# Layer norm sums over partitions on GpSimd instead of a fold, a split and a product, and a ScalarE/GpSimd mix for the first tile's receptance

## The chip, the cores and the metric

The kernel runs on one NeuronCore of a Trainium2 chip. The metric is the device time of one execution in microseconds (us); the median of three runs of the kernel before is 1569.22 us (1567.82 to 1571.45). TensorE multiplies matrices into PSUM, VectorE and ScalarE do elementwise work, GpSimd does elementwise work on SBUF and issues DMAs, and SyncE only issues DMAs. Each engine executes its own instructions in the order in which they were built.

## The reference, cut to what matters

The input x is [2, 4096, 256]. Features lie on partitions (two blocks of 128), time on the free axis. The block is a layer norm, an RWKV attention, a second layer norm and a gated feed-forward of four weight matrices:

```python
def _layernorm(x, axis=-1, eps=1e-05):
    m = jnp.mean(x, axis=axis, keepdims=True)
    v = jnp.var(x, axis=axis, keepdims=True)
    return (x - m) / jnp.sqrt(v + eps)
...
xr = x * time_mix_r + x_prev * (1.0 - time_mix_r)      # likewise xk, xv
r = jax.nn.sigmoid(jnp.einsum('btd,ed->bte', xr, W_r))  # likewise k, v
y = r * _wkv_scan(k, v, time_decay, time_first)
x = x + jnp.einsum('btd,ed->bte', y, W_o)
...
h = silu(lin(z, w1)) * lin(z, w2)          # z = layernorm(x), 256 -> 1024
h = gelu(lin(h, h1)); h = gelu(lin(h, h2))  # 1024 -> 1024, twice
x = x + lin(h, w3)                          # 1024 -> 256
```

Since features lie on partitions, the mean and the variance of a layer norm are sums over partitions.

## The kernel before, in words

There are 16 tiles of 512 time steps. The feed-forward `ffn(i)` of tile i is woven with the attention of tile i+1 (`attention`) and the first layer norm of tile i+2 (`normalise`): all are generators, and the main loop advances them step by step. A scheduler of the framework then gives each engine its final order. The first tile has a hand-written order instead (`first_tile`): `on(...)` puts every instruction behind the last one of its engine.

Feed-forward products are split: each activation is a rounded part `hi` and a rest `lo`, and every weight block is multiplied by both (lines 172 and 173). A first-layer block f makes two PSUM tiles `pa` and `pb`. ScalarE applies Silu to `pa` (L564), VectorE multiplies by `pb` (`gated`, L565), ScalarE rounds (`hi`, L179) and VectorE subtracts (`lo`, L180). PSUM pool `ps_ffn` has four buffers, so `pb` of block f+2 takes the buffer of `pb` of block f and can start only when L565 of block f has read it. In the two middle layers ScalarE reads PSUM twice (L580, L582) and VectorE makes `lo` (L583).

A layer norm takes two partition sums, each made by `average` in five instructions: VectorE adds the two feature blocks (`both`, L187); ScalarE moves the upper 64 partitions down (`folded`, L189); VectorE adds the halves (L192); ScalarE rounds (`hi` of `parts`, L194) and VectorE makes the rest (L197); then one product with a matrix of 1/256 (L201) gives the average in every partition, in PSUM. Then L212 subtracts the mean, L215 squares, a second `average` and L218 give the standard deviation, L220 the reciprocal, L222 the product.

There are four such sums in every tile but the first, 60 in all. The first tile has its own layer norm (`first_layernorm`), and it scales the weights (`scaled`) so that its k, v and r projections need no mixed input: each takes four products per half of the features.

GpSimd's queue issues the casting weight loads at the start, `h2` to a rounded copy in HBM in eight pieces and `w3` among them (L123, L124), the loads of x (L95), the stores of the output (L604) and the loads for comparing the rounded weights (L152).

Of the kernel before, what the change touches and what calls it, by code (L numbers as in the profile page):

```python
# [7 lines left out]

F32 = mybir.dt.float32
F32R = mybir.dt.float32r  # L10
# [3 lines left out]
P = 128  # L14
B, T, D, HID = 2, 4096, 256, 1024
TS = 512
# [49 lines left out]
def split_block(ctx, tc, flags, x, vecs, w_attn, w1, w2, h1, h2, w3, out):  # L66
# [52 lines left out]
    h2_hbm = dram.tile([NH, P, NH, P], F32R, name="h2_hbm")  # L119
    for sb, src in ((w1_sb, w1), (w2_sb, w2), (h1_sb, h1)):  # L120
        nc.gpsimd.dma_start(out=sb, in_=src)
    for f in range(NH):
        nc.gpsimd.dma_start(out=h2_hbm[f], in_=h2[:, :, f * P : (f + 1) * P])  # L123
    nc.gpsimd.dma_start(out=w3_sb, in_=w3)  # L124

    mean_w = const.tile([P, P], F32, name="mean_w")
    vector.memset(mean_w, 1.0 / D)
# [51 lines left out]
        marks["rounded"] = scalar.activation(hi, full, AF.Copy)  # L179
        marks["rest"] = vector.tensor_tensor(lo, full, hi.bitcast(F32), ALU.subtract)  # L180

    def average(a, b, tag, name, pause=False):

        both = one.tile([P, TS], F32, tag=tag, name="both")
        marks["both"] = vector.tensor_tensor(both, a, b, ALU.add)  # L187
        folded = one.tile([P // 2, TS], F32, tag="folded", name="folded")
        marks["shift"] = scalar.activation(folded, both[P // 2 :, :], AF.Copy)  # L189
        if pause:  # L190
            yield
        marks["fold"] = vector.tensor_tensor(folded, folded, both[: P // 2, :], ALU.add)  # L192
        parts = one.tile([P, TS], F32R, tag="parts", name="parts")
        marks["hi"] = scalar.activation(parts[: P // 2, :], folded, AF.Copy)  # L194
        if pause:
            yield
        marks["split"] = vector.tensor_tensor(parts[P // 2 :, :], folded, parts[: P // 2, :].bitcast(F32), ALU.subtract)  # L197
        if pause:
            yield
        psum = ps_sum.tile([P, TS], F32, tag="ps", name=name)  # L200
        marks["average"] = tensor.matmul(psum, mean_wr, parts, start=True, stop=True)  # L201
        return psum

    def layernorm(src, new_xc, tag, pause=False):


        mean = yield from average(src[:, 0, :], src[:, 1, :], tag, "mean", pause)
        if pause:
            yield
        xc = new_xc()  # L210
        for h in range(ND):
            vector.tensor_tensor(xc[:, h, :], src[:, h, :], mean, ALU.subtract)  # L212
        yield
        sq = wide.tile([P, ND, TS], F32, tag="wide", name="sq")
        scalar.activation(sq, xc, AF.Square)  # L215
        var = yield from average(sq[:, 0, :], sq[:, 1, :], tag, "var")
        rstd = one.tile([P, TS], F32, tag=tag, name="rstd")
        scalar.activation(rstd, var, AF.Sqrt, bias=eps)  # L218
        yield
        vector.reciprocal(rstd, rstd)  # L220
        for h in range(ND):
            vector.tensor_tensor(xc[:, h, :], xc[:, h, :], rstd, ALU.mult)  # L222
        yield
# [126 lines left out]
    def add(out, a, b, op=ALU.add):  # L350
        on("vector", "tensor_tensor", out, a, b, op)

    def load_sqrt_table():
        activation(root, eps, AF.Sqrt)

    def keep_warm(unread, n, size=TS):

# [6 lines left out]
    def first_layernorm(src, xc, means):  # L364

        sq = wide.tile([P, ND, TS], F32, tag="wide", name="sq")
        for mean, p in zip(means, halves):
            for h in range(ND):  # L370
                add(xc[:, h, p], src[:, h, p], mean, ALU.subtract)
            activation(sq[:, :, p], xc[:, :, p], AF.Square)
        varis = []
        for p in halves:
            add(sq[:, 0, p], sq[:, 0, p], sq[:, 1, p])
            var = ps_ffn.tile([P, TS // 2 // P], F32, tag="pf", name="var")
            for b in range(TS // 2 // P):
                t = slice(p.start + b * P, p.start + (b + 1) * P)
                matmul(var[:, b : b + 1], sq[:, 0, t], mean_w[:, 0:1], start=True, stop=True)
            varis.append(var)  # L380
        yield
        spread = []
        for var in varis:
            each = tmp.tile([P, TS // 2 // P], F32, tag="each", name="each")
            activation(each, var, AF.Sqrt, bias=eps)
            on("vector", "reciprocal", each, each)
            rstd = ps_ffn.tile([P, TS // 2], F32, tag="pf", name="rstd")
            for b in range(TS // 2 // P):
                matmul(
                    rstd[:, b * P : (b + 1) * P], each[:, b : b + 1].to_broadcast([P, P]), ident, start=True, stop=True  # L390
                )
            spread.append(rstd)
            yield
        for rstd, p in zip(spread, halves):
            for h in range(ND):
                add(xc[:, h, p], xc[:, h, p], rstd, ALU.mult)
            yield

    def first_tile(second):
# [13 lines left out]
                    both = one.tile([P, 2, TS], F32, tag=tag, name="scale")  # L413
                    scales.append([both[:, k, :] for k in range(2)])

        load_sqrt_table()
        unread = ps_sum.tile([P, TS], F32, tag="ps", name="unread")
        keep_warm(unread, 8)
        means = []
# [6 lines left out]
        norm = first_layernorm(x_sb, xn, means)  # L426


        scaled = [[hid.tile([P, ND, D], F32, tag=tag, name="ws") for tag in ("hi", "lo")] for m in range(3)]

        def scale(m, *which):
            for k, c in which:
# [1 line left out]
                activation(scaled[m][k][:, c, :], wa_sb[:, m, c, :], AF.Copy, scale=(vec, unmix)[k][:, j : j + 1])  # L434

        next(norm)
        scale(0, (0, 0))
        next(norm)
        scale(0, (1, 0))
        next(norm)  # L440
        scale(0, (1, 1), (0, 1))
        for m in range(1, 3):
            scale(m, (0, 0), (1, 0), (1, 1), (0, 1))
        run(norm)
        nc.gpsimd.tensor_copy(prev, xn[:, :, TS - 1 :])

        def project(m, h, kind, p=whole):
            pool, tag = kind
            ps = pool.tile([P, p.stop - p.start], F32, tag=tag, name="ps_" + "kvr"[m])
            now, then = (ws[:, :, h * P : (h + 1) * P] for ws in scaled[m])  # L450
            skip = 1 if p.start == 0 else 0
            shifted = slice(p.start + skip - 1, p.stop - 1)
            matmul(ps, now[:, 0, :], xn[:, 0, p], start=True, stop=False)
            for c in range(ND):
                matmul(ps[:, skip:], then[:, c, :], xn[:, c, shifted], start=False, stop=False)
            matmul(ps, now[:, 1, :], xn[:, 1, p], start=False, stop=True)
            return ps
# [6 lines left out]
        def differences(h):  # L464
# [5 lines left out]
                on("vector", "scalar_tensor_tensor", sc[h][1][:, p], t, w, k, ALU.add, ALU.subtract)  # L470
                on("vector", "scalar_tensor_tensor", so[h][1][:, p], k, u, t, ALU.add, ALU.subtract)
            on("vector", "tensor_scalar", sc[h][0], sc[h][1], NEG_CLAMP, 0.0, ALU.max, ALU.min)
            nc.gpsimd.tensor_copy(log_max[:, h : h + 1], lm[h][:, TS:])

        def scales(h):
            activation(sc[h][0], sc[h][0], AF.Exp)
            activation(sc[h][1], sc[h][1], AF.Relu)
            activation(sc[h][1], sc[h][1], AF.Exp, scale=-1.0)

        def state(h):  # L480

            on("vector", "scalar_tensor_tensor", sc[h][1], sc[h][1], MIN_SCALE, v[h], ALU.max, ALU.mult)
            on("vector", "tensor_tensor_scan", num[h][:, 1:], sc[h][0], sc[h][1], num[h][:, 0:1], ALU.mult, ALU.add)
            nc.gpsimd.tensor_copy(numer[:, h : h + 1], num[h][:, TS:])
            for share, of in zip(so[h], (num[h][:, 0:TS], v[h])):
                on("vector", "scalar_tensor_tensor", share, share, MIN_SHARE, of, ALU.max, ALU.mult)
            add(so[h][0], so[h][0], so[h][1])

        differences(0)
        with behind("vector"), behind("scalar"):  # L490
            next(second)
        last["vector"], last["scalar"] = marks["both"], marks["shift"]
        scales(0)
        with behind("vector"), behind("scalar"):
            next(second)
        last["vector"], last["scalar"] = marks["fold"], marks["hi"]
        differences(1)
        scales(1)
        for h in range(ND):
            activation(so[h][0], so[h][1], AF.Sigmoid, scale=-1.0)  # L500
            activation(so[h][1], so[h][1], AF.Sigmoid)
        for h in range(ND):
            activation(r[h], r[h], AF.Sigmoid)
            state(h)
        load_sqrt_table()

        with behind("vector"):
            next(second)
        last["vector"] = marks["split"]
        y = wide.tile([P, ND, TS], F32, tag="wide", name="y")  # L510
        add(y[:, 0, :], so[0][0], r[0], ALU.mult)
        for p in halves:
            add(y[:, 1, p], so[1][0][:, p], r[1][:, p], ALU.mult)
        banks = [
            [pool.tile([P, TS // 2], F32, tag=tag, name="ps_o") for pool, tag in kinds]
            for kinds in ((attn, attn), (attn, ffn))
# [6 lines left out]
        for ps_of, p in zip(banks, halves):  # L523
# [2 lines left out]
                add(x_sb[:, h, p], x_sb[:, h, p], ps_of[h])  # L526
                matmul(mean, mean_w, x_sb[:, h, p], start=h == 0, stop=h == ND - 1)
            means.append(mean)
        with behind("tensor"):
            next(second)  # L530
        last["tensor"] = marks["average"]
        unread = ps_attn.tile([P, TS], F32, tag="pa", name="unread")
        keep_warm(unread, 4)
        x2 = wide.tile([P, ND, TS], F32, tag="wide", name="x2")
        x2_hi = one.tile([P, ND, TS], F32R, tag="x2_hi", name="x2_hi")
        x2_lo = one.tile([P, ND, TS], F32R, tag="x2_lo", name="x2_lo")
        norm = first_layernorm(x_sb, x2, means)
        for _ in range(3):
            next(norm)
        keep_warm(unread, 6)  # L540
        run(norm)
# [79 lines left out]
    normal, got = {}, {}  # L621
    second = normalise(1)
    first_tile(second)
    for i in range(len(tiles)):
        ahead = attention(i + 1) if i + 1 < len(tiles) else iter(())
        further = normalise(i + 2) if i + 2 < len(tiles) else iter(())
        for step, _ in enumerate(ffn(i, *got.pop(i))):
            if i == 0:
                if step in (1, NH - 1):
                    with tc.issue_after(marks["rounded"].ins), tc.issue_after(marks["rest"].ins):  # L630
                        next(second)
                elif step == NH:
                    run(second)
# [287 lines left out]
```

## Time and profile before

| what | value |
|---|---|
| median of 3 runs | 1569.22 us |
| the profiled execution | 1570.85 us, its span 1569.1 us |
| TensorE busy | 1559.1 us, 99% |
| VectorE busy | 1102.3 us, 70% |
| ScalarE busy | 1035.0 us, 66% |
| GpSimd busy | 60.0 us, 4% |
| granted TensorE clock | 0.998 |

A row of a group gives the line, the engine, the operation, the tiles, the count, the busy time, the mean duration, and the idle time of the engine before it with what ended that idle time. Matrix products are pipelined: their modelled durations overlap, so the distance from start to start says what one costs, not the duration in the row. In a timeline the columns are start, duration, engine, line, operation, tiles and, in brackets, the idle time before.

### The profile page before, as it was taken

Reading aid. Unit: us, or ns where it says so; the run is one execution under the profiler, and the core shown is the slowest. Engines: PE = TensorE matmul, PEld = TensorE weight load, DVE = VectorE, ACT = ScalarE, POOL = GpSimd, SP = SyncE. Lnnn points to the kernel's source line nnn. Section 1 sums busy time; section 2 is a strip of 40 time slices with the busy share of each in tenths; the row PEclk is TensorE's granted clock in tenths of the full one; section 3 lists DMA queues with packets and bytes.
Section 4 is the critical chain, followed back from the end, with each engine's and each line's share of the span. In section 5 each row is a group of like instructions: output and inputs, shape, how many; then the busy total and the mean of one; then the engine's idle time right before and its main releaser. Section 6 shows DMA issues by size and latency. Waiting matters only on the chain.

```text
span 1569.1 us, 16653 instructions
## 1 busy us (share of the span) xinstructions
PE 1559.1 (99%) x6319; PEld 1184.3 (75%) x6319; DVE 1102.3 (70%) x1763; ACT 1035.0 (66%) x1394; POOL 60.0 (4%) x98
## 2 busy tenths in 40 slices
PE   9999999999999999999999999999999999999998
PEld 6768777777777778777787777877777777777886
DVE  6788686776768768787676867768677676865531
ACT  5686767667577585776757767676776757756542
POOL 3000000000000000000000000000000000000000
PEclk9999999999999999999999999999999999999999
DMA  9113030220312203022130311203112030210302
GB/s 356 47 31 105 14 121 34 68 94 7 124 39 69 86 20 127 22 81 74 31 125 14 104 51 45 97 14 108 35 60 88 8 116 32 67 61 21 107 0 83
DMA packets 36887, 109.16 MB, mean 70 GB/s; under 512 B 3713, under 2 KB 12673, under 8 KB 36289
## 3 DMA queue, kind: packets, MB, share of 16 engines
q1 hardware_dynamic: 19424, 68.32, 13.4%
q0 software_dynamic: 16816, 39.07, 8.1%
q8 instruction: 51, 0.84, 0.2%
q10 hardware_dynamic: 560, 0.66, 0.1%
q14 instruction: 36, 0.29, 0.1%
HBM read 99.64 MB, written 12.58 MB: 72 GB/s over the span
## 4 chain that ended last, share of the span: by engine, by line
PE 97%; DVE 2%; DMA 1%; ACT 0%; issue 0%; DVEq 0%; POOLq 0%
PE ph L172 30%; PE ph L173 30%; PE po L173 4%; PE po L172 4%; PE pb L172 4%; PE pa L172 4%; PE pb L173 4%; PE pa L173 4%; PE ps_k L165 3%; PE ps_r L165 3%; PE ps_v L165 3%; PE ps_o L165 3%; PE mean L201 1%; PE var L201 1%; DVE scale L342 0%; DMA out<-x_sb 0%
## 5 line engine op out<-in xcount | busy, mean ns | idle before, releaser
L172 PE MATMUL ph<-hi,h_sb 128*128 128x512 f32 x2048 | 813.4, 397 | 0.0
L173 PE MATMUL ph<-lo,h_sb 128*128 128x512 f32 x2048 | 800.8, 391 | 0.0
L172 PEld LDWEIGHTS ph<-hi,h_sb 128*128 128x128 f32 x2048 | 384.7, 188 | 93.3 <-issue 11.7
L173 PEld LDWEIGHTS ph<-lo,h_sb 128*128 128x128 f32 x2048 | 384.6, 188 | 88.8 <-issue 8.4
L583 DVE TENSOR_TENSOR lo<-full,hi 128x512 fp32r<-128x512 f32 x256 | 175.4, 686 | 173.2 <-ACT full L582 172.2
L580 ACT ACTIVATE hi<-ph,vec 128x512 fp32r<-128x512 f32 x256 | 175.9, 687 | 183.4 <-PE ph L173 182.0
L582 ACT ACTIVATE full<-ph,vec 128x512 f32<-128x512 f32 x256 | 174.5, 682 | 0.9 <-DVE lo L583 0.8
L565 DVE SCALAR_TENSOR_TENSOR gated<-pb,vec,gated 128x512 f32<-128x512 f32 x128 | 95.4, 748 | 58.0 <-PE pb L173 31.0
L580 ACT ACT_TABLE_LOAD x102 | 130.9, 1283 | 1.8
L564 ACT ACTIVATE gated<-pa,vec 128x512 f32<-128x512 f32 x128 | 86.5, 684 | 59.4 <-PE pa L173 56.2
L220 DVE RECIPROCAL rstd<-rstd 128x512 f32<-128x512 f32 x30 | 100.4, 3346 | 5.3 <-ACT rstd L218 5.3
L172 PE MATMUL pb<-x_hi,w_sb 128*128 128x512 f32 x256 | 102.0, 398 | 0.7 <-DVE gated L565 0.7
L172 PE MATMUL pa<-x_hi,w_sb 128*128 128x512 f32 x256 | 101.9, 398 | 0.1
L173 PE MATMUL pb<-x_lo,w_sb 128*128 128x512 f32 x256 | 100.6, 393 | 0.0
L173 PE MATMUL pa<-x_lo,w_sb 128*128 128x512 f32 x256 | 100.6, 393 | 0.0
L173 PE MATMUL po<-lo,w_sb 128*128 128x512 f32 x256 | 100.2, 392 | 0.0
L172 PE MATMUL po<-hi,w_sb 128*128 128x512 f32 x256 | 100.0, 391 | 0.0
L179 ACT ACTIVATE hi<-gated 128x512 fp32r<-128x512 f32 x128 | 80.5, 629 | 27.9 <-DVE gated L565 26.5
L180 DVE TENSOR_TENSOR lo<-gated,hi 128x512 fp32r<-128x512 f32 x128 | 87.7, 686 | 5.3 <-ACT hi L179 0.7
L248 DVE TENSOR_TENSOR_SCAN lm<-vec,lm,ps_k 128x512 f32<-128x512 f32 x30 | 38.3, 1278 | 42.9 <-PE ps_k L165 42.8
L303 DVE SCALAR_TENSOR_TENSOR mx<-xn,vec,mx 128x512 f32<-128x512 f32 x90 | 66.5, 745 | 0.3
L595 DVE SCALAR_TENSOR_TENSOR x_sb<-po,vec,x_sb 128x512 f32<-128x512 f32 x32 | 24.0, 751 | 59.0 <-PE po L173 59.0
(144 smaller groups left out, 1811.3 us busy)
## 6 DMA issues: line engine op xcount, KB each, us to landing
h_sb<-h_hbm SPq DMA_DIRECT2D x128, 512.0 KB, 3.3
raw<-in_h POOLq DMA_DIRECT2D x32, 256.0 KB, 3.1
x_sb<-in_x POOLq DMA_DIRECT2D x15, 512.0 KB, 4.0
out<-x_sb POOLq DMA_DIRECT2D x15, 512.0 KB, 3.1
h_sb<-in_h POOLq DMA_DIRECT2D x1, 4096.0 KB, 19.7
h_hbm<-in_h POOLq DMA_DIRECT2D x8, 512.0 KB, 24.7
w_sb<-in_w POOLq DMA_DIRECT2D x3, 1024.0 KB, 10.5
raw<-in_w POOLq DMA_DIRECT2D x12, 256.0 KB, 2.8
```

Source lines behind the costliest of these rows:

```text
L165: tensor.matmul(psum, weights(c), src[c], start=c == 0, stop=c == n - 1)
L172: tensor.matmul(psum, weights(c), hi, start=c == 0, stop=False)
L173: tensor.matmul(psum, weights(c), lo, start=False, stop=c == n - 1)
L179: marks["rounded"] = scalar.activation(hi, full, AF.Copy)
L180: marks["rest"] = vector.tensor_tensor(lo, full, hi.bitcast(F32), ALU.subtract)
L220: vector.reciprocal(rstd, rstd)
L303: vector.scalar_tensor_tensor(mx[:, h, :], xn[:, h, 1:], vec[:, j : j + 1], mx[:, h, :], ALU.mult, ALU.add)
L564: scalar.activation(full, pa, AF.Silu, scale=col(S1, f))
L565: vector.scalar_tensor_tensor(full, pb, col(S2, f), full, ALU.mult, ALU.mult)
L580: scalar.activation(hi, ps, AF.Gelu, scale=col(scales, f))
L582: scalar.activation(full, ps, AF.Gelu, scale=col(scales, f))
L583: vector.tensor_tensor(lo, full, hi.bitcast(F32), ALU.subtract)
```

## The change

`average` goes. `total` makes the sum of the two blocks as before and then one GpSimd instruction, a sum over all partitions that leaves the result in every partition, in SBUF. The factor 1/256 moves into the subtraction of the mean (now a `scalar_tensor_tensor`) and into the scale of the square root. In the first tile the receptance input is mixed before the product: ScalarE scales the tile and the tile one step earlier, GpSimd adds them, and the r projection takes two products per half in place of four. The second tile's first partition sum moves behind the first tile's `y`. The state step is cut in two (`state`, `result`). The Exp table is loaded earlier. The first tile's small GpSimd copies go through `on`, and the loads of `h2` and `w3` are issued behind them. The second step of tile 1's layer norm moves from step NH - 1 to NH - 2 of the first feed-forward.

```diff
-    for f in range(NH):
-        nc.gpsimd.dma_start(out=h2_hbm[f], in_=h2[:, :, f * P : (f + 1) * P])
-    nc.gpsimd.dma_start(out=w3_sb, in_=w3)
+    def load_rest():
+        for f in range(NH):
+            nc.gpsimd.dma_start(out=h2_hbm[f], in_=h2[:, :, f * P : (f + 1) * P])
+        nc.gpsimd.dma_start(out=w3_sb, in_=w3)
...
-    def average(a, b, tag, name, pause=False):
+    def total(a, b, tag):
         both = one.tile([P, TS], F32, tag=tag, name="both")
         marks["both"] = vector.tensor_tensor(both, a, b, ALU.add)
-        folded = one.tile([P // 2, TS], F32, tag="folded", name="folded")
-        marks["shift"] = scalar.activation(folded, both[P // 2 :, :], AF.Copy)
-        marks["fold"] = vector.tensor_tensor(folded, folded, both[: P // 2, :], ALU.add)
-        parts = one.tile([P, TS], F32R, tag="parts", name="parts")
-        marks["hi"] = scalar.activation(parts[: P // 2, :], folded, AF.Copy)
-        marks["split"] = vector.tensor_tensor(parts[P // 2 :, :], folded, parts[: P // 2, :].bitcast(F32), ALU.subtract)
-        psum = ps_sum.tile([P, TS], F32, tag="ps", name=name)
-        marks["average"] = tensor.matmul(psum, mean_wr, parts, start=True, stop=True)
-        return psum
+        everywhere = one.tile([P, TS], F32, tag="total", name="total")
+        nc.gpsimd.partition_all_reduce(everywhere, both, channels=P, reduce_op=ReduceOp.add)
+        return everywhere
...
-            vector.tensor_tensor(xc[:, h, :], src[:, h, :], mean, ALU.subtract)
+            vector.scalar_tensor_tensor(xc[:, h, :], mean, -1.0 / D, src[:, h, :], ALU.mult, ALU.add)
...
-        scalar.activation(rstd, var, AF.Sqrt, bias=eps)
+        scalar.activation(rstd, var, AF.Sqrt, bias=eps, scale=1.0 / D)
...
+        mx, then = (wide.tile([P, ND, TS], F32, tag="wide", name="mx") for _ in range(2))
+        for c in range(ND):
+            j = 2 * ND + c
+            activation(mx[:, c, :], xn[:, c, :], AF.Copy, scale=vec[:, j : j + 1])
+            activation(then[:, c, 1:], xn[:, c, : TS - 1], AF.Copy, scale=unmix[:, j : j + 1])
+            on("gpsimd", "tensor_tensor", mx[:, c, 1:], mx[:, c, 1:], then[:, c, 1:], ALU.add)
+        load_table(AF.Exp)
...
+            if m == 2:
+                for c in range(ND):
+                    matmul(ps, wa_sb[:, 2, c, block], mx[:, c, :], start=c == 0, stop=c == ND - 1)
+                return ps
...
+        state(0)
+        result(0)
+        state(1)
+        add(y[:, 0, :], so[0][0], r[0], ALU.mult)
+        result(1)
+        for p in halves:
+            add(y[:, 1, p], so[1][0][:, p], r[1][:, p], ALU.mult)
+        with behind("vector"), behind("scalar"):
+            next(second)
...
+    with behind("gpsimd"):
+        load_rest()
...
-                if step in (1, NH - 1):
+                if step in (1, NH - 2):
```

## The prediction

> **What bounds the kernel now.** I read the page's busy times and chain first, then the groups, then timelines of one steady tile.
>
> ```profile
> PE 1559.1 (99%) x6319; PEld 1184.3 (75%) x6319; DVE 1102.3 (70%) x1763; ACT 1035.0 (66%) x1394; POOL 60.0 (4%) x98
> PE 97%; DVE 2%; DMA 1%; ACT 0%; issue 0%; DVEq 0%; POOLq 0%
> L201 PE MATMUL mean<-parts,mean_wr 128*128 128x512 f32 x30 | 18.6, 622 | 0.1
> L201 PE MATMUL var<-parts,mean_wr 128*128 128x512 f32 x30 | 18.0, 599 | 0.0
> ```
>
> TensorE ends the kernel: 97% of the chain. A product taken from its stream is a gain in full, and a stall of its stream is a loss in full, since no later slack takes it back. VectorE and ScalarE idle for 30% and more, so their removed work counts only where TensorE waits for it.
>
> TensorE's timeline at one of these products, from 774 us:
>
> ```profile
> 773.97 0.39 PE L173 MATMUL ph<-lo,h_sb 128*128 128x512 f32 x1
> 774.20 0.39 PE L172 MATMUL ph<-hi,h_sb 128*128 128x512 f32 x1
> 774.65 1.88 PE L165 MATMUL ps_o<-y,wa_sb 128*128 128x512 f32 x4
> 775.97 0.79 PE L201 MATMUL var<-parts,mean_wr 128*128 128x512 f32 x1
> 776.60 1.88 PE L165 MATMUL ps_o<-y,wa_sb 128*128 128x512 f32 x4
> ```
>
> The durations overlap; starts tell the cost. A `ph` product takes 0.23 us (774.20 less 773.97). Four `ps_o` passes and one L201 take 776.60 - 774.65 = 1.95 us; four such passes alone take 1.72 us elsewhere, so L201 costs 0.23 us, not its mean of 0.6.
>
> **Part 1, the sums leave TensorE.** 60 products of L201 by 0.23 us: **13.8 us off the path**. VectorE loses L192 and L197 (60 x 1.36 us), ScalarE L189 and L194 (60 x 1.25 us): off the path, counted at nothing. The mean's subtraction becomes a scalar_tensor_tensor, 0.75 us for 0.68 us (rows L303 and L212), hidden in VectorE's idle time except where part 3 counts it.
>
> **Part 2, the first tile.** The r projection halves from 16 passes of 0.43 us to 8, so TensorE ends it at about 29.4 us, not 32.8. Its new input is four ScalarE scalings (0.6 us each, from about 12 us, when `xn` is complete; six weight scalings of 0.45 us go) and two GpSimd adds of 511 columns, 1 to 2 us each by the GpSimd rows below. It is ready by 18 us and needed at 25.8 us: hidden by the k and v products; without that cover the four microseconds of adds would show. What sets the end here is VectorE:
>
> ```profile
> 32.61 0.69 DVE L197 TENSOR_TENSOR parts<-folded,parts 64x512 fp32r<-64x512 f32 x1
> 33.33 1.35 DVE L342 TENSOR_TENSOR y<-scale,ps_r 128x512 f32<-128x512 f32 x3
> 36.53 1.72 DVE L342 TENSOR_TENSOR x_sb<-x_sb,ps_o 128x256 f32<-128x256 f32 x4 [1.86 <-PE ps_o L342]
> 34.07 3.72 PE L342 MATMUL ps_o<-y,wa_sb 128*128 128x256 f32 x16 [1.24 <-DVE y L342]
> ```
>
> `parts` (0.69 us) leaves the line before `y`, L187 and L192 leave the one before the second key scan (0.4 us net, and as much on ScalarE), two small copies of 0.15 us enter. The second block's first half of `y` then ends near 33.4 us instead of 34.4. In the built order the first block of `y` now stands ahead of the second block's result, so its eight `ps_o` passes (1.8 us) are done when 33.4 comes; two passes (0.45) and 0.2 of delay later the first add could start, and the moved `both` (0.68) holds VectorE until 34.5. 36.53 - 34.5: **2.0 us gained**. At least 0.7 us if `ps_o` stays as it is.
>
> GpSimd's queue: nine issues of `load_rest` (0.75 us each) now start at about 31 us. The second tile's first sum stands behind five of them, at about 35.5 us; its reader stands in the first feed-forward's third block, near 50 us, so 10 us of sum and start are hidden. `h2` is first multiplied after 192 feed-forward products of 0.23 us, past 89 us, some 50 us after its loads. SyncE's three prefetches of it, issued at 25.3 us before, wait longer for nobody.
>
> **Part 3, where the new sum is waited for.** Its duration, L, is the one number this case turns on, and no row shows it. In the built order of the changed kernel I looked at all four places per tile. The variance of the first norm has the other head's scan and products of 8 us ahead of its reader on ScalarE. The second norm's two sums stand in the second middle layer, where VectorE then waits L less a few tenths, and ScalarE for the variance. Queued behind are `lo` and Gelu work of a layer whose block takes 16 x 0.23 = 3.7 us: four PSUM and three `full` buffers give two blocks, over 7 us, and the old five-instruction path took 6 us there (782.4 to 788.4). Counted at nothing for L below 6. The fourth place is tight: from tile 3 on, 13 times, the mean's sum stands in the first feed-forward layer, whose block takes 1.87 us.
>
> VectorE's timeline of that layer before, and the same layer one tile later when the load of x came late:
>
> ```profile
> 814.22 0.75 DVE L565 SCALAR_TENSOR_TENSOR gated<-pb,vec,gated 128x512 f32<-128x512 f32 x1 [1.17 <-PE pb L173]
> 821.08 0.69 DVE L187 TENSOR_TENSOR both<-x_sb 128x512 f32<-128x512 f32 x1
> 821.68 0.68 DVE L180 TENSOR_TENSOR lo<-gated,hi 128x512 fp32r<-128x512 f32 x1
> 822.29 0.74 DVE L565 SCALAR_TENSOR_TENSOR gated<-pb,vec,gated 128x512 f32<-128x512 f32 x1
> ...
> 918.68 0.69 DVE L187 TENSOR_TENSOR both<-x_sb 128x512 f32<-128x512 f32 x1 [1.90 <-DMA x_sb<-in_x]
> 919.89 0.74 DVE L565 SCALAR_TENSOR_TENSOR gated<-pb,vec,gated 128x512 f32<-128x512 f32 x1
> 920.69 0.50 PE L172 MATMUL pb<-x_hi,w_sb 128*128 128x512 f32 x1 [0.70 <-DVE gated L565]
> ```
>
> The reader is to see that 1.90 us of VectorE waiting already cost TensorE about 0.86 us: `pb` waits for L565 two blocks earlier, 0.80 us from the start of `gated` to the start of `pb`. Now count from the first `gated` (814.22 = 0). `both` ends at 7.55, GpSimd starts at 7.65 (ScalarE follows it 0.07 us later in the trace), the sum ends at 7.65 + L. Behind `both` the changed order has `lo` and `gated` of block 4, done by 8.8, then the subtraction, which waits, and **behind it `gated` of block 5**. That starts 0.07 + 0.66 us after the sum, and `pb` of block 7 0.80 us later: 9.18 + L. Unhindered it starts at 11.86 (in the later tile, whose 0 is 909.84, at 921.70). The stall is L - 2.68, plus about 0.1 for the last `lo` of the layer.
>
> What is L? The nearest GpSimd rows:
>
> ```profile
> 0.74 0.20 POOL L107 MEMSET ident<- 128x128 f32 x1 [0.29 <-POOLq L914]
> 2.23 0.31 POOL L108 TENSOR_SCALAR_AFFINE_SELECT ident<-ident 128x128 f32<-128x128 f32 x1
> ```
>
> A pass over 512 columns at their pace takes 0.8 to 1.24 us: one pass is the lower end. The upper end is the Trainium skill, "GPSIMD Engine Reference", section 3.2: a reduction along partitions of [128, 2048] took 247.7 us, so 61.9 us for 512 columns, an estimate, if the new instruction works like that one. I take **4.0 us**, five passes of 0.8: four halvings of a core's 16 partitions (128 over 8 cores, by the same page) and one exchange between cores. It is nearer the lower rows[...].
>
> A rule speaks against the change. The row has the `lo` at 821.68, which reads two SBUF tiles, begin just before GpSimd would. The Trainium skill, "SBUF — State Buffer", section "Who interferes with whom", says that a VectorE instruction with two SBUF inputs and a GpSimd one that reads SBUF exclude each other for their whole length, the first to start winning. No row before has a large GpSimd read, so nothing here shows it. By the rows alone the stall is 4.0 - 2.68 + 0.1 = 1.42 us, 13 times 18.5. By the rule GpSimd starts after that `lo`, at 8.2, and the stall is 1.97 us, 13 times **25.6 us**. I take the rule.
>
> **The sum.** From the profiled execution's 1570.85 us (span 1569.1 and 1.75 around it): -13.8 - 2.0 + 25.6 = 1580.7; the profiled one lies 1.6 above the median, so **1579** for the median; without the rule 1572.
>
> **The rivals.** (a) The sum is short. At L below 3.0 the stall is under one microsecond a tile, at 2.0 nothing, and the time is 1569.2 - 15.8 = **1553**, faster. For it: the pace of one pass; against it: sixteen lanes and eight cores have to be joined. It decides where 13 x (L - 2.03) equals 15.8, at L = 3.25 us. (b) About equal, L from 3.0 to 3.5: 1566 to 1572. (c) GpSimd becomes the bound. At L = 10 the first-layer stall alone is 13 x 8.0 = 104 us, **1657**; at 61.9 us, 60 sums make **3700**. Against it: nothing but my count of passes. (d) The stalls are hidden but part 2 fails, or a tile's `ps_o` waits for a scan held by the lock: some 5 to 10 us, 1572 to 1580; `y` has about 3 us to spare (770.5 against 774.0).
>
> **How the numbers follow.** Likeliest, L from 3.5 to 6: 0.45, its own range 1573 to 1606. (a) 0.27, (b) 0.10, (c) 0.14, (d) 0.04. A measurement of this kernel can tell about 0.2%, 3.1 us, from no change. Faster 0.27, same 0.10, slower 0.63. The range reaches from (a)'s 1553 to 1612, L of 6.5; beyond it lie most of (c) and a little below 1553.
>
> **What would show it.** Rows of the GpSimd sum of about 4 us; `pb` of the first feed-forward layer waiting for `gated`, once a tile, 1 to 2 us; no L201 rows; the first feed-forward product near 42.9 us in place of 44.9. I am wrong if the sums take under 3 us, or if they take 4 us and `pb` does not wait.

## The result and the profile after

| | before | after |
|---|---|---|
| median | 1569.25 us (1567.82 to 1571.45, 5 runs) | 1590.35 us (1588.76 to 1591.95, 5 runs) |
| profiled span | 1569.1 us | 1588.6 us |
| TensorE products | 6319 | 6253 |
| GpSimd busy | 60.0 us | 263.8 us |

The ratio is 1.0132, 95% interval 1.0121 to 1.0143: 21 us slower. The forecast was 10 us slower (1579), so the sign and the range held, and the size did not.

From the page of the kernel after: busy times, the chain that ended last by engine, and the groups that answer to those shown of before (columns: busy, mean ns of one, idle time just before them and what ended most of it).

```profile
PE 1550.2 (98%) x6253; PEld 1175.7 (74%) x6253; DVE 1072.0 (67%) x1643; ACT 967.4 (61%) x1274; POOL 263.8 (17%) x160
PE 85%; DVE 6%; POOL 4%; issue 3%; DMA 1%; ACT 1%; POOLq 0%; DVEq 0%
L175 PE MATMUL ph<-hi,h_sb 128*128 128x512 f32 x2048 | 819.9, 400 | 9.1 <-DMA h_sb<-h_hbm 9.0
L190 POOL PARTITION_ALL_REDUCE total<-both x60 | 201.1, 3352 | 509.6 <-DVE both L188 334.3
L175 PE MATMUL pb<-x_hi,w_sb 128*128 128x512 f32 x256 | 103.1, 403 | 8.9 <-DVE gated L564 8.9
L176 PE MATMUL po<-lo,w_sb 128*128 128x512 f32 x256 | 101.4, 396 | 2.2 <-DVE lo L582 2.2
```

The same three groups of TensorE on the page of the kernel before:

```profile
L172 PE MATMUL ph<-hi,h_sb 128*128 128x512 f32 x2048 | 813.4, 397 | 0.0
L172 PE MATMUL pb<-x_hi,w_sb 128*128 128x512 f32 x256 | 102.0, 398 | 0.7 <-DVE gated L565 0.7
L173 PE MATMUL po<-lo,w_sb 128*128 128x512 f32 x256 | 100.2, 392 | 0.0
```

TensorE fell from 97% to 85% of the chain, and these three groups now wait: 9.1, 8.9 and 2.2 us where they waited 0.0, 0.7 and 0.0. `pb` for `gated` was forecast. `ph` for the streamed blocks of h2, and `po` for `lo`, were not. A sum takes 3.23 us where nothing disturbs it (minimum 3.228, median 3.242; the row's mean of 3.35 holds the disturbed ones too), where the forecast took 4.0.

**The forecast stall**, in a plain tile (timeline of VectorE, GpSimd and TensorE together):

```profile
844.33 0.69 DVE L183 TENSOR_TENSOR lo<-gated,hi 128x512 fp32r<-128x512 f32 x1
844.59 3.52 POOL L190 PARTITION_ALL_REDUCE total<-both  x1 [4.51 <-DVE both L188]
848.14 0.69 DVE L201 SCALAR_TENSOR_TENSOR xn<-total,x_sb 128x512 f32<-128x512 f32 x1 [2.47 <-POOL total L190]
848.75 0.75 DVE L564 SCALAR_TENSOR_TENSOR gated<-pb,vec,gated 128x512 f32<-128x512 f32 x1
849.55 0.50 PE L175 MATMUL pb<-x_hi,w_sb 128*128 128x512 f32 x1 [0.67 <-DVE gated L564]
```

The sum ends at 848.11; the subtraction starts 0.03 later, `gated` 0.61 after it, `pb` 0.80 after that. That is the chain that the forecast counted (0.07 + 0.66 + 0.80).

**The stall nobody counted**, in the feed-forward of tile 3 (the first tile is 0). VectorE's, GpSimd's, SyncE's and TensorE's timelines after:

```profile
407.94 0.69 DVE L188 TENSOR_TENSOR both<-x_sb 128x512 f32<-128x512 f32 x1
408.80 3.23 POOL L190 PARTITION_ALL_REDUCE total<-both  x1 [15.69 <-DVE both L188]
412.06 1.29 DVE L201 SCALAR_TENSOR_TENSOR x<-total,x_sb 128x512 f32<-128x512 f32 x2 [3.36 <-POOL total L190]
415.54 2.86 DVE L291 TENSOR_SCALAR mx<-xn,unmix 128x512 f32<-128x512 f32 x2
415.79 3.32 POOL L190 PARTITION_ALL_REDUCE total<-both  x1 [3.76 <-DVE both L188]
418.99 1.53 POOL L155 DMA_DIRECT2D raw<-in_h  x2
422.29 0.69 DVE L157 SCALAR_TENSOR_TENSOR raw<-raw,h_sb 128x512 f32<-128x512 f32 x1 [0.47 <-DMA raw<-in_h]
423.15 0.69 DVE L157 SCALAR_TENSOR_TENSOR raw<-raw,h_sb 128x512 f32<-128x512 f32 x1 [0.17 <-DMA raw<-in_h]
423.88 0.32 SPq L575 DMA_DIRECT2D h_sb<-h_hbm  x1
...
427.22 0.77 PE L175 MATMUL ph<-hi,h_sb 128*128 128x512 f32 x1 [3.01 <-DMA h_sb<-h_hbm]
427.78 0.63 PE L176 MATMUL ph<-lo,h_sb 128*128 128x512 f32 x1
428.20 0.63 PE L175 MATMUL ph<-hi,h_sb 128*128 128x512 f32 x1
```

VectorE's timeline of the same place before:

```profile
399.27 0.63 DVE L187 TENSOR_TENSOR both<-x_sb 128x512 f32<-128x512 f32 x1
...
406.46 0.68 DVE L154 SCALAR_TENSOR_TENSOR raw<-raw,h_sb 128x512 f32<-128x512 f32 x1
...
407.46 0.68 DVE L154 SCALAR_TENSOR_TENSOR raw<-raw,h_sb 128x512 f32<-128x512 f32 x1
408.07 0.69 DVE L187 TENSOR_TENSOR both<-sq 128x512 f32<-128x512 f32 x1
```

In tiles 1 to 8 of the loop VectorE compares one streamed block of h2 with the matrix as given, in two instructions (L154 before, L157 after). Only then is the block's stream buffer free, and there are three. Before, the second comparison ended 8.9 us after the start of `both`, and ahead of the second sum. After, it ended 15.9 us after `both`, behind two sums: VectorE waits 3.36 us for the first, `mx` takes 2.86 us instead of 0.87 under the second, and the raw loads are issued behind both sums on GpSimd's queue. The next block's load is issued at 423.88, 0.04 us after the second comparison ends, and lands at 427.08; TensorE, whose last product had started at 423.82, goes on at 427.22. Behind that wait, products start 0.43 us apart (427.78, 428.20) instead of 0.23, some twelve of them: another 2.4 us.

**Where the 19.5 us of the span come from.** The distance from one tile's first `pb` to the next's, an interval, gives the budget. A plain tile, one without the waits for h2 and `po`, took 95.62 us before and 95.43 after. The kernel `late` below, in which `pb` does not wait, needs 94.35 for it. TensorE waits nowhere in the plain tile before. So the four products were worth 95.62 - 94.35 = 1.27 us per tile, and the stall 95.43 - 94.35 = 1.08, of which 0.83 shows as the start of `pb` and the rest as slightly later starts around it.

| term | forecast | measured, from the starts |
|---|---|---|
| products gone | -13.8 | 15 tiles x 1.27 = -19.1 |
| first tile | -2.0 | +1.5 (first product at 46.32, not 44.86) |
| `pb` behind the late sum | +25.6 | 13 x 1.08 = +14.0 |
| second tile | 0 | +6.9 (first interval: 97.62 before, 103.23 after, and 1.27 for the products) |
| h2 stream and `po`, behind comparisons | 0 | +16.4 |

The last row is the excess of the later intervals over a plain tile, 18.0 us after less 1.6 before. The sum is 19.7; the last tile's end gives 0.2 back.

In the first interval `ps_v`, a product of the second tile's attention, waits 2.95 us for VectorE. The same place in the kernel after and in `stream4` below:

```profile
95.93 3.78 PE L168 MATMUL ps_v<-mx,wa_sb 128*128 128x512 f32 x4 [2.95 <-DVE so L255]
95.95 3.07 PE L168 MATMUL ps_v<-mx,wa_sb 128*128 128x512 f32 x4 [2.96 <-DVE so L255]
```

The eight passes of `ps_v` and `ps_r` behind this wait take 6.2 us up to the next `ph` (102.09) in the kernel after and 4.8 in `stream4` (100.79). This is why the first interval is 103.23 us in this one trace and 101.6 to 101.9 in most of the kernels below, with the comparisons or without: 1.3 us of the second tile's 6.9 come and go with it.

### The profile page after: what moved, and what is told of

It is laid out like the page before. It is cut to its first block, busy times and chain, and to the rows that moved or that the text cites. A ratio compares the mean times of both kernels' runs of the same rounds, so it can differ in the third digit from the quotient of the medians.

```text
span 1588.6 us, 16466 instructions
## 1 busy us (share of the span) xinstructions
PE 1550.2 (98%) x6253; PEld 1175.7 (74%) x6253; DVE 1072.0 (67%) x1643; ACT 967.4 (61%) x1274; POOL 263.8 (17%) x160
## 4 chain that ended last, share of the span: by engine, by line
PE 85%; DVE 6%; POOL 4%; issue 3%; DMA 1%; ACT 1%; POOLq 0%; DVEq 0%
PE ph L176 27%; PE ph L175 27%; POOL total L190 4%; PE po L176 4%; PE po L175 4%; PE ps_v L168 3%; PE ps_o L168 3%; PE ps_r L168 3%; PE ps_k L168 3%; PE pb L175 3%; PE pb L176 3%; PE pa L175 2%; PE pa L176 2%; DVE gated L564 1%; DMA h_sb<-h_hbm 1%
## 5 line engine op out<-in xcount | busy, mean ns | idle before, releaser
L176 PE MATMUL ph<-lo,h_sb 128*128 128x512 f32 x2048 | 809.7, 395 | 0.0
L190 POOL PARTITION_ALL_REDUCE total<-both x60 | 201.1, 3352 | 509.6 <-DVE both L188 334.3
L291 DVE TENSOR_SCALAR mx<-xn,unmix 128x512 f32<-128x512 f32 x90 | 69.4, 800 | 0.0
```

Of the source, the lines that this page charges most:

```text
L176: tensor.matmul(psum, weights(c), lo, start=False, stop=c == n - 1)
L190: nc.gpsimd.partition_all_reduce(everywhere, both, channels=P, reduce_op=ReduceOp.add)
```

## The experiments

Ratios are to the kernel before, measured beside each kernel.

**The two parts apart.** `first_alone` keeps the first tile's new order and the moved loads, with the old five-step sum in `total`:

```diff
-        everywhere = one.tile([P, TS], F32, tag="total", name="total")
-        nc.gpsimd.partition_all_reduce(everywhere, both, channels=P, reduce_op=ReduceOp.add)
-        return everywhere
+        scalar.activation(folded, both[P // 2 :, :], AF.Copy)
...
+        tensor.matmul(psum, mean_wr, parts, start=True, stop=True)
+        return psum
```

> The changed kernel with the old five-step sums (copy, add, copy, subtract, product) in place of the GpSimd sum, so the first tile's new order alone. Theory: the loss is made by the GpSimd sums and by what comes with them; without them the late write of ident (13.21 us in the changed kernel, 2.23 before) is back near 2.2 us, the rstd products of the first tile wait 4.2 us less, and the predicted gain of part 2 appears: first feed-forward product near 43 us in place of 44.86, and 1566.5 to 1567.5 us, 0.998 to 0.999 of before. Rival: the first tile's new order is itself what costs the start (46.32 us) and tile 1; then the first feed-forward product stays near 46 us and the time is 1571 to 1576 us.

Measured: 1566.77 us, ratio 0.9982 (0.9976 to 0.9989). `sums_alone` is the opposite: before, with `total` in place of `average`.

> The kernel before with the GpSimd sums put in place of fold, split and product; its first tile and its order of loads stay. Theory: the thirteen first-layer stalls of 0.8 us and the waits of the h2 stream stay, the products' 13.8 us are gained, and the late ident costs the start about 4 us without the first tile's gain of 2.7: 1588 to 1595 us, 1.012 to 1.016 of before. Rival: the loss comes from the first tile's new order or from the load order moved behind it; then this kernel is near 1569 - 14 + 11 = 1566 us.

Measured: 1588.73 us, ratio 1.0115 (1.0098 to 1.0132). The sums alone make the loss, and the first tile's new order alone gains. From GpSimd's and TensorE's timelines of `first_alone`:

```profile
2.23 0.31 POOL L109 TENSOR_SCALAR_AFFINE_SELECT ident<-ident 128x128 f32<-128x128 f32 x1
9.28 1.29 PE L337 MATMUL rstd<-ident,each 128*128 128x128 f32 x8
42.60 0.39 PE L175 MATMUL pa<-x_hi,w_sb 128*128 128x512 f32 x1
```

and from those of the kernel after:

```profile
13.21 0.28 POOL L109 TENSOR_SCALAR_AFFINE_SELECT ident<-ident 128x128 f32<-128x128 f32 x1 [11.09 <-issue]
13.55 2.08 PE L331 MATMUL rstd<-ident,each 128*128 128x128 f32 x8 [4.20 <-POOL ident L109]
48.15 3.25 POOL L190 PARTITION_ALL_REDUCE total<-both  x1 [9.36 <-issue]
```

Part 2 alone starts the feed-forward at 42.60 us; the forecast said 42.9. With the sums in the program, GpSimd stands idle for 11.09 us ("issue": no wait that the profile shows) ahead of the affine_select that writes `ident`, and 9.36 us ahead of the first sum, whose input was ready. The first tile's `rstd` products wait 4.20 us for `ident`.

**The comparisons.** The raw loads and VectorE's comparison are left out of the kernel after, and out of the kernel before as a control:

```diff
-        nc.gpsimd.dma_start(out=raw, in_=given)
...
-        vector.scalar_tensor_tensor(raw, raw, 1.0, kept.bitcast(F32), ALU.mult, ALU.not_equal, ...)
+    vector.memset(rounded, 0.0)
```

> The changed kernel without the comparisons of the operands as given with the rounded ones: the raw loads and VectorE's L157 are left out, the counter of differences is set to 0. Theory: the h2 stream's buffers come free only when a comparison is done, its raw load stands behind the sums on GpSimd's queue, and TensorE waits for the stream: 16 us of the 21 us come from there, so this kernel takes 1573 to 1576 us, and the waits of ph for h_sb (9.1 us on the page) are gone. Rival: these waits are made by the transfers or by contention of SBUF, not by the comparisons; then they stay, and the time falls by less than 4 us.

> Control: the kernel before without the same comparisons and raw loads, the counter set to 0. Theory: before, the comparisons are hidden (ph waits 0.0 us for h_sb), so the time changes by 2 us at most: 1567 to 1570 us. Rival: the comparisons cost TensorE as much before; then it falls by 10 us or more, and they explain nothing of the difference.

Measured: 1572.44 us, ratio 1.0016 (1.0007 to 1.0025), and 1567.83 us, ratio 0.9988 (0.9981 to 0.9995). Leaving the comparisons out is worth 18 us after and 2.5 us before; 1.3 of the 18 are the first interval above, which is short in other kernels too. The group of `ph` in `after_no_compare`, beside the one of `pb`:

```profile
L171 PE MATMUL ph<-hi,h_sb 128*128 128x512 f32 x2048 | 817.3, 399 | 0.0
L171 PE MATMUL pb<-x_hi,w_sb 128*128 128x512 f32 x256 | 103.1, 403 | 9.8 <-DVE gated L560 9.8
```

The stream's wait is gone, and the forecast stall is untouched: two separate causes.

**What makes the comparisons late?** First the queue: `raw_sync` issues the raw loads on SyncE.

```diff
-        nc.gpsimd.dma_start(out=raw, in_=given)
+        nc.sync.dma_start(out=raw, in_=given)
```

> The changed kernel with the raw loads of the comparisons issued from SyncE's queue in place of GpSimd's; the comparisons stay. Theory: the raw loads are late because they stand behind the sums on GpSimd's queue; moved, the waits of ph for h_sb and of po for lo are gone and the time is that without the comparisons, 1572 to 1576 us, 16 us less than the changed kernel. Rival: the comparisons' VectorE work or their traffic, not the queue, makes the waits; then less than 4 us is gained, and 1586 to 1590 us remains; or SyncE's queue itself stalls the stream behind a raw load, and the waits move there (1580 or more).

Measured: 1586.61 us, ratio 1.0110 (1.0094 to 1.0125). My theory fell: `ph` still waits 9.2 us, and only `po`'s wait shrinks, from 2.2 to 0.6 us. VectorE's and SyncE's timelines of this kernel, in the same tile:

```profile
408.38 4.71 SPq L155 DMA_DIRECT2D raw<-in_h  x2
410.37 1.29 DVE L201 SCALAR_TENSOR_TENSOR x<-total,x_sb 128x512 f32<-128x512 f32 x2 [3.35 <-POOL total L190]
419.35 0.68 DVE L157 SCALAR_TENSOR_TENSOR raw<-raw,h_sb 128x512 f32<-128x512 f32 x1
419.96 3.35 DVE L209 RECIPROCAL rstd<-rstd 128x512 f32<-128x512 f32 x1
```

The raw loads are issued by 413.1 now, and the first comparison still runs at 419.35, without waiting for its load: it stands on VectorE behind both sums, and the second one (423.23) behind the 3.35 us reciprocal too. New theory: the place on VectorE. `half` makes half as many comparisons per tile, in twice as many tiles; `stream4` leaves them where they are and gives the stream a fourth buffer:

```diff
-                if layer == 1 and i == f + 1:
+                if layer == 1 and i in (f + 1, f + NH - 1):
...
-                    for c in range(0, NH, n):
+                    for c in (0,) if i == f + 1 else (n,):
```

```diff
-    hid = ctx.enter_context(tc.tile_pool(name="hid", bufs=16))
-    stream = ctx.enter_context(tc.tile_pool(name="stream", bufs=3))
+    hid = ctx.enter_context(tc.tile_pool(name="hid", bufs=15))
+    stream = ctx.enter_context(tc.tile_pool(name="stream", bufs=4))
```

> The changed kernel with one comparison of a streamed block per tile in place of two: the first half of block f in tile f+1, the second in tile f+7, so tiles 7 and 8 have two, of different blocks. Theory: it is where the comparison stands on VectorE, not how much VectorE does there, that holds the buffer: the buffer of tiles 3 to 5 comes free less than a microsecond earlier, and new waits of the same kind appear in tiles 9 to 11: 1587 to 1597 us. Rival: the 1.4 us of comparison work, and the two raw loads, are what is late; then half of the loss is gone and the second halves cost nothing: 1580 to 1584 us.

> The changed kernel with four buffers in place of three for the streamed blocks of h2, paid for by 15 in place of 16 hidden buffers of each kind; the comparisons stay as they are, raw loads on GpSimd's queue. Moving the raw loads alone gave back only 3.7 us of the 18 that leaving the comparisons out gave. Theory: the comparisons of tiles 3 to 5 stand on VectorE behind the second norm's waits for its two sums (3.4 us, and 2 us more under the second sum), so a stream buffer comes free some 5 to 9 us late; a fourth buffer gives one block (16 x 0.23 = 3.7 us) of slack, so most of the 10 us of ph waits for h_sb and the cold products behind them are gone: 1576 to 1581 us. The 4 us around tile 8, where po waits for lo behind a comparison, stay. Rival: the transfers themselves are slowed by the sums or by the raw loads; then the waits stay, 1587 to 1591 us.

> The changed kernel with 15 in place of 16 hidden buffers of each kind, nothing else: the control for the kernels with four stream buffers. Theory: the freed buffer was never waited for, since its last reader is the last product of the layer before: 1589 to 1592 us, as the changed kernel. Rival: the order of work changes with it and removes waits; then part of the 12.7 us that four stream buffers gained is its own.

Measured: `half` 1587.72 us, ratio 1.0116 (1.0101 to 1.0132); `stream4` 1577.64 us, ratio 1.0046 (1.0030 to 1.0061); `hid15`, the control with 15 hidden buffers alone, 1587.54 us, ratio 1.0115 (1.0099 to 1.0131). The control lies 2.8 us below the kernel after, with overlapping intervals of the ratio, and its `ph` waits 9.0 us as there; in its trace 0.8 us of this are an earlier first `pb` and 1.4 the first interval. So 10 to 13 us belong to the fourth buffer (1577.64 against 1587.54 and against 1590.35). In `stream4` and in `half`, the group of `ph`:

```profile
L175 PE MATMUL ph<-hi,h_sb 128*128 128x512 f32 x2048 | 817.5, 399 | 2.2 <-DMA h_sb<-h_hbm 2.2
```

```profile
L175 PE MATMUL ph<-hi,h_sb 128*128 128x512 f32 x2048 | 819.5, 400 | 11.4 <-DMA h_sb<-h_hbm 11.4
```

With half the work per tile the wait is not smaller but spread over ten places, up to tile 10, where it had been four in tiles 2 to 4. With one block (3.7 us) of slack all but one place is covered. So it is how late on VectorE the comparison stands, not its work and not its traffic.

**The first-layer stall.** `late` builds the subtraction behind the last `lo` of the first layer, from tile 2 on:

```diff
+        with tc.issue_after(marks["rest"].ins) if late else nullcontext():
             for h in range(ND):
                 vector.scalar_tensor_tensor(xc[:, h, :], mean, -1.0 / D, src[:, h, :], ALU.mult, ALU.add)
...
-        yield from layernorm(x_sb, new_xn, "rstd1", pause=i == 1)
+        yield from layernorm(x_sb, new_xn, "rstd1", pause=i == 1, late=i > 1)
```

> The changed kernel with the mean's subtraction of the first norm, from tile 2 on, put behind the last lo of the first feed-forward layer, so that no gated of that layer stands behind it on VectorE. Theory: the 13 waits of pb for gated (0.8 us each, 8.9 us on the page, 11 us in starts) are gone, and nothing else: 1578 to 1581 us. Rival: the stalls are made by VectorE being held while GpSimd works, wherever the subtraction stands; then pb still waits and the time stays within 3 us of 1590.

Measured: 1573.23 us, ratio 1.0028 (1.0019 to 1.0037).

```profile
L175 PE MATMUL pb<-x_hi,w_sb 128*128 128x512 f32 x256 | 101.9, 398 | 0.0
```

`pb` waits for nothing, and 17 us come back where 11 were expected: 14.0 us are the 1.08 per tile in place of the 0.83 that the start of `pb` shows. The rest is 0.5 at the start, 1.6 in the first interval and 1.1 in the tile shown above (101.6 to 99.3, less the 1.08). The first two are no work of this edit: `hid15` has them as well. The third was not expected and not taken apart.

**The start.** `ident_dma` writes `ident` by VectorE, and by three DMAs on ScalarE's queue; `best` has this edit, `late`, `raw_sync` and an earlier variance sum of tile 1 together.

```diff
-    nc.gpsimd.memset(ident, 0.0)
-    nc.gpsimd.affine_select(...)
+    nc.scalar.dma_start(out=rows, in_=seed[:, : P + 1])
+    nc.scalar.dma_start(out=rows[:, 0:1], in_=seed[:, P + 1 :])
+    nc.scalar.dma_start(out=ident, in_=flat[: P * P].rearrange("(p q) -> p q", q=P))
```

> The changed kernel with ident written by VectorE and three DMAs on ScalarE's queue in place of GpSimd's memset and affine_select. Theory: the first tile's rstd products wait 4.2 us for ident, because affine_select runs 11 us later than before; with ident there by 12 us or earlier the first feed-forward product starts near 43 us in place of 46.3, and 1586 to 1588 us remains. Rival: the next in line, the rstd chain's other inputs or the k and v operands, is as late; then the start moves by less than 1 us.

> All three edits in the changed kernel (raw loads on SyncE's queue, the late subtraction, ident without GpSimd), and the second tile's variance sum in the third block earlier of the first feed-forward layer (step 4 in place of 6). Theory: the causes are separate and add up: 1590.35 - 16.5 - 11 - 4.2 - up to 4.8 = 1554 to 1560 us, below the kernel before by 10 us or more, the 13.8 us of the products being kept. Rival: the recovered stalls come back elsewhere (SyncE's queue, VectorE's holds, the second norm's waits); then 1563 us or more.

Measured: 1602.31 us, ratio 1.0204 (1.0189 to 1.0220), and 1583.10 us, ratio 1.0088 (1.0074 to 1.0102). Both missed, for a reason of my edit: the three DMAs depend on each other, landed after 6.9, 11.7 and 4.0 us among the weight loads, and ScalarE stood behind them. The first `pb` came at 58.5 us, so the 12 us of this edit hide what `best` gained. A second try, `ident_sync`, uses two DMAs on SyncE's queue, in the combined kernel below.

> The same fastest kernel with ident written by VectorE to memory and read back by two DMAs at the end of SyncE's first loads; ScalarE's queue stays free, GpSimd does not run affine_select. Theory: if ident lands by 10 us the rstd products no longer wait 4 us and the first feed-forward product starts near 43 us: 1554 to 1556 us; the gap before the first sum (9.4 us) stays. Rival: the DMAs are as late as GpSimd was, behind the weight loads that now start at once (a DMA of the same size landed after 6.9 us in the earlier try); then the start moves by less than 1 us or is later, 1558 us or more.

Measured: 1570.62 us, ratio 1.0003 (0.9995 to 1.0011), 12 us above the kernel that it was built from. From TensorE's timeline:

```profile
24.63 2.05 PE L334 MATMUL rstd<-ident,each 128*128 128x128 f32 x8 [15.20 <-DMA ident<-flat]
58.74 0.39 PE L177 MATMUL pb<-x_hi,w_sb 128*128 128x512 f32 x1
```

This edit gained nothing either, but it gives a third point on one line. `rstd` products at 9.28, 13.55 and 24.63 us go with a first `pb` at 42.83, 46.66 and 58.74: 4.3 us later costs 3.8, and 11.1 later costs 12.1. In all 14 kernels with the new first tile the first `pb` comes 33.1 to 34.5 us after the `rstd` products. So the start hangs on `ident` one for one, within about a microsecond, and that accounts for the missing gain of part 2.

**Together.** `late_stream4` joins the two edits that worked, `late_stream4_sync` adds the raw loads on SyncE, and `tile1` also moves the variance sum of tile 1 from step 6 to step 4 of the first layer (`if step in (1, 4):`).

> The late subtraction and the four stream buffers in the changed kernel together; ident and the raw loads stay. Theory: the two stalls are separate and their gains add: 17.1 us for the first (measured), 10 to 14 for the second: 1559 to 1563 us, below the kernel before, with some 4 us left in tile 8, 4 in the start and 5 in tile 1. Rival: with one stall gone VectorE is later elsewhere and the other grows; then 1566 us or more.

> The same with the raw loads on SyncE's queue too. Theory: the raw loads no longer stand behind a sum, so po's wait in tile 8 (2.2 us and cold products behind it) is gone as well: 3 to 4 us below the kernel without this edit, 1555 to 1560 us. Rival: on SyncE's queue a raw load that waits for its buffer holds back the stream of h2, as in the kernel with this edit alone; then it is no faster than without it.

> The fastest kernel so far (late subtraction, four stream buffers, raw loads on SyncE's queue: 1558.3 us) with the variance sum of tile 1 two blocks earlier in the first feed-forward layer. Theory: the first interval is 101.9 us, 7.6 above the others, because tile 1's k and v products wait for that sum's chain (1.7 and 3.1 us); two blocks (3.7 us) earlier the waits shrink by 2 to 4.5 us: 1554 to 1556.5 us. Rival: the chain then waits for VectorE in the first layer instead (in the kernel with all edits new waits of 1.5 us stood there): 1557 to 1559 us.

| kernel | median, us | ratio, 95% |
|---|---|---|
| `late_stream4` | 1561.81 | 0.9950 (0.9936 to 0.9963) |
| `late_stream4_sync` | 1558.32 | 0.9925 (0.9912 to 0.9939) |
| `tile1` | 1556.23 | 0.9909 (0.9894 to 0.9924) |

From the page of `late_stream4_sync`:

```profile
PE 94%; DVE 4%; issue 1%; POOL 1%; ACT 0%; DMA 0%; POOLq 0%; DVEq 0%
L175 PE MATMUL ph<-hi,h_sb 128*128 128x512 f32 x2048 | 817.4, 399 | 0.0
L175 PE MATMUL pb<-x_hi,w_sb 128*128 128x512 f32 x256 | 102.0, 398 | 0.0
```

Both causes are gone, every interval from the second on is 94.3 to 94.6 us, but for 95.6 in tile 7, where `po` still waits 1.0 us, and with the sums still on GpSimd the kernel is 0.75% faster than before. `tile1` takes 1.8 us off the first interval (101.9 to 100.1); its time's interval overlaps with that of `late_stream4_sync`. New waits of 0.60 and 0.61 us stand in the first tile's first middle layer, as the rival said, so the second tile's 6.9 us are explained in part only. The first interval was 2.0 us above a plain tile before, and is still 5.8 above here.

## Why the prediction was right and wrong

- **The first-layer stall: right in mechanism, a term mis-sized.** It is in the place named, 13 times, with the starts counted. L was taken as 4.0 us; it measured 3.23. The same working at 3.23, with the rule, makes 13 x 1.20 = 15.6 in place of 25.6; measured, 14.0.
- **The rule on shared access: half right.** The sum started without delay at 844.59 but took 3.52 us instead of 3.23 while `lo` ran. It cost 0.29 us, not the 0.55 that the forecast added.
- **Part 1: undersized.** The forecast took 0.23 us per product, from starts on either side of one product. In the period of a whole tile it is 0.32 (1.27 / 4), so 19.1 us, not 13.8. What the products cost beside their own starts was not taken apart.
- **Part 2: right alone, wrong in this program.** The forecast's working for the first tile gave 42.9, and alone it is 42.60. The step that failed is the silent one, that GpSimd's affine_select stays at the 2.23 us of the row it quoted; it came at 13.21, and the first tile lost 1.5 us where 2.0 were to be gained. A new kind of instruction on GpSimd was costed where it stands, and not by what it does to the others in the same program.
- **Part 3, "counted at nothing for L below 6": the main failure.** The step foresaw VectorE waiting "L less a few tenths" at the second norm, listed `lo` and Gelu work as queued behind it, and stopped. Behind that wait stand also the comparisons, and behind those a stream buffer, a load, and TensorE: 16.4 us where nothing was counted. For the first layer the prediction had named all that is queued behind the waiting instruction and who waits for that; here it did not, and the comparisons, which run in half of the tiles, are not in it.
- **The second tile, counted at nothing:** 6.9 us. The `load_rest` step asked only whether the sum of its mean is ready in time. `ps_k` waits 1.5 us for `mx` and `ps_v` 3.0 us for `so`, both VectorE's work in the second tile's attention, behind its norm. Moving its variance sum two blocks earlier gave back 1.8, so that sum is a part of it; the rest of this term stays open.
- **Rival (a)'s threshold** was L = 3.25 us for no change. L came out at 3.23 and the kernel was 21 us slower, which is the plainest sign that the sum lacked terms.
- **That the sign came out right was luck.** With the L that was measured the forecast's own sum makes 15.6 - 13.8 - 2.0, no change. An L taken too long stood in for the terms that were left out.

## What to carry to other kernels

When an instruction starts to wait, list everything behind it on its engine over all kinds of iteration, the rare ones too, and follow each item to the buffer that it frees: here a check that runs in eight tiles of sixteen cost more than the stall in thirteen. A product's or a stall's worth is best read from the period of a whole iteration, not from the starts beside it. And an operation moved to an idle engine may be cheaper to keep there and repair around (a later reader, one more buffer) than to take back: the repaired kernel is 0.75% faster than the original, where the plain move was 1.3% slower. Part of this is the first tile's new order, which alone gives 0.2%. The repairs were not tried in the original; leaving its comparisons out altogether took 2.5 us off it, and the repaired kernel lies 9.5 us below that.

## What the hardware showed unexpectedly

**GpSimd idles about ten microseconds, twice, in a program that has both affine_select and the sum.** In the traces of kernels with both, affine_select came at 11.7 to 13.2 us after 9.5 to 11.1 us of idle "issue"; without sums it came at 2.23. Without affine_select the gap at the start is gone, and 9.1 to 10.5 us of it still stand before the first sum. The Trainium skill ("GPSIMD Engine Reference", section 2.1) gives about 6 us for the first call of newly loaded code, with no row in the profile; the missing row agrees, the time here is half as long again or more. That these gaps are such loads is inferred: no row names them, and why affine_select has no gap in programs without the sum stays open. The forecast did not budget it.

**A sum holds VectorE for about 2.0 of its 3.2 us, and not every instruction.** VectorE's timeline beside GpSimd's, twice in the kernel after:

```profile
291.73 3.23 POOL L190 PARTITION_ALL_REDUCE total<-both  x1 [8.78 <-DVE lm L228]
292.25 2.80 DVE L251 TENSOR_TENSOR_SCAN num<-sc,num 128x512 f32<-128x512 f32 x1
...
317.63 3.52 POOL L190 PARTITION_ALL_REDUCE total<-both  x1 [2.36 <-DVE both L188]
317.99 2.46 DVE L291 TENSOR_SCALAR mx<-xn,unmix 128x512 f32<-128x512 f32 x1
320.36 0.68 DVE L157 SCALAR_TENSOR_TENSOR raw<-raw,h_sb 128x512 f32<-128x512 f32 x1
```

The scan takes 1.29 us elsewhere (its median) and ends at 295.05; less its own time that is 293.76, 2.03 us after the sum began. `mx` (0.48 elsewhere) reads one tile only and is held too: its end less its own time is 319.97, 2.34 us after the start of a sum that took 3.52, 0.29 more than an undisturbed one. The comparison at 320.36, with two SBUF inputs, runs at its usual 0.68 us while the sum still has 0.79 us to go. In the plain tile `gated`, which reads PSUM and SBUF, started at 844.93, 0.34 us into a sum, and took its usual 0.75 us. The rule that the prediction drew on (the Trainium skill, "SBUF — State Buffer", "Who interferes with whom") has the two exclude each other for the whole length of the instruction; here it was about the first two thirds, and the measurement decides.
